# Second layer of a two-layer graph kernel: values stationary on column halves, normalisation on GpSimd, projections issued beside attention

## Chip, cores, metric

One core of one Trainium2 chip. The metric is the device time of one execution in microseconds (us); lower is better. The record marks each run as fast or slow; all runs quoted are marked fast.

## The reference

64 batches of 256 nodes with 512 features, fp32, one adjacency matrix for all. Each layer is x + f(relu(layernorm(x))), and the two layers follow each other:

```python
# layer 1 of the program ("first layer"): graph attention with additive logits, one head
Wh = h @ W
logits = leaky_relu(Wh @ a_src [rows] + Wh @ a_dst [columns], 0.2)
out = softmax(logits where adj else -inf) @ Wh
# layer 2 ("second layer"): masked attention, 8 heads of 64
q, k, v = h @ Wq.T + bq, h @ Wk.T + bk, h @ Wv.T + bv
scores = q @ k.T / 8, masked by adj
out = (softmax(scores) @ v) @ Wo.T + bo
```

## The kernel before

The kernel works on groups of two batches (4 tiles of 128 tokens), 32 groups. The first layer of the next group is issued among the second layer of this group. On each engine the program order is fixed when the kernel is built.

Names in the profiles: PE is TensorE, DVE VectorE, ACT ScalarE, POOL GpSimd, SP the engine that issues the transfers. `pw`, `pq`, `pk`, `pv` are the products with W, Wq, Wk, Wv; `po` the output products, and on its own line the first layer's value product; `pt` the transposes of the normalised x; `pp` those of probabilities; `psc` the scores; `pav` the second layer's values. A bank is one buffer of the `ps_` pools, to which TensorE writes its results. The parts that the change touches:

```python
ps_tr = ... tile_pool(name="ps_tr", bufs=3, space=PSUM)     # transposes
ps_sc = ... tile_pool(name="ps_sc", bufs=3, space=PSUM)     # scores
# ... cut ...
def values(t, hq, pr):                      # four heads of one tile
    # ... cut: pav is one bank of ps_mm, 128 tokens x 512 columns ...
    for i in range(2):
        pp = ps_tr.tile(...)
        # ... cut: transposes of two heads' probabilities into pp ...
        if i: nc.scalar.copy(pT, pp)
        else: nc.vector.tensor_copy(pT, pp)
        for r in range(2):
            h = hq * HQ + 2 * i + r
            for kc in range(NC):            # probabilities stationary, 64 columns of v move
                nc.tensor.matmul(pav[:, h*DH:(h+1)*DH], pT[:, r, kc, :],
                                 v[:, b*NC+kc, h*DH:(h+1)*DH], ...)

def finish(t):
    rc = 1 / sm                             # reciprocal sums, after the values
    nc.vector.tensor_mul(av, pav, rc ...)
    # ... cut: four transposes of av into pa, copy to aT ...
    project_rows(po, aT, wo_sb, 0)
    # ... cut: add to x, write out ...

for g in range(G):
    # ... cut ...
    for n, _ in enumerate(layer1(g)):       # norm, q, k, v, then attention of group g
        if n % 5 != 4:
            next(ahead, None)               # first layer of group g + 1
    run(ahead)
```

Of the kernel before, what the change touches and what calls it, by code (L numbers as in the profile page):

```python
# [8 lines left out]
F32 = mybir.dt.float32  # L9
# [15 lines left out]
def kernel(  # L25
# [17 lines left out]
    """Two pre-norm residual layers over batches of N nodes, kept on chip between them:  # L43
    graph attention with additive logits, then masked multi-head attention.

    A group is two batches, i.e. NT = 4 tiles of 128 tokens; its first layer is issued
    among the second layer of the group before it.
    """
# [17 lines left out]
    ps_tr = ctx.enter_context(tc.tile_pool(name="ps_tr", bufs=3, space=PSUM))  # L66
    ps_sc = ctx.enter_context(tc.tile_pool(name="ps_sc", bufs=3, space=PSUM))
# [47 lines left out]
    # 0 where there is an edge, MASKED where there is none  # L115
# [5 lines left out]
    def norm_relu_T(xt, g, layer):  # L121
        """relu(layernorm(x)) with the features on the partitions: [P, DC, TOK]."""
# [10 lines left out]
        yield  # L133
        hT = big.tile([P, DC, TOK], F32, tag="hT", name=f"hT{nm}")
        for t in range(NT):
            xn = work.tile([P, D], F32, tag="xn", name=f"xn{nm}_{t}")
            nc.vector.tensor_scalar(
                xn, xt[:, t, :], mv[:, t, 0:1], rstd[:, t : t + 1], op0=ALU.subtract, op1=ALU.mult
            )
            pt = ps_tr.tile([P, DC, P], F32, tag="tr", name=f"pt{nm}_{t}")  # L140
            for c in range(DC):
                nc.tensor.transpose(pt[:, c, :], xn[:, c * P : (c + 1) * P], ident)  # L142
            nc.scalar.activation(hT[:, :, t * P : (t + 1) * P], pt, AF.Relu)  # L143
            yield
        return hT

    def project_rows(dst, hT, w_t, t):
        """dst[tokens of tile t, all columns] = h @ w_t"""
# [5 lines left out]
    def project_T(dst, hT, w_t, e):  # L154
        """dst[columns of chunk e, all tokens] = (h @ w_t).T"""
# [5 lines left out]
    def layer0(g):  # L161
# [3 lines left out]
        wh = big.tile([P, NT, D], F32, tag="wh", name=f"wh_{g}")  # L165
        es = small.tile([P, NT], F32, tag="es", name=f"es_{g}")
        ed = small.tile([P, NT], F32, tag="ed", name=f"ed_{g}")
        for t in range(NT):
# [3 lines left out]
            for dst, a in ((ed, a_dst_b), (es, a_src_b)):  # L172
                junk = work.tile([P, D], F32, tag="junk", name=f"junk_{g}_{t}", bufs=2)
# [3 lines left out]
            yield  # L177

        prob, rec = {}, {}
        for b in range(GB):  # L180
# [22 lines left out]
            # a row without an edge gives 0  # L203
# [4 lines left out]
            yield  # L208

        for b in range(GB):  # L210
# [22 lines left out]
            yield  # L233

    def layer1(g):
        xt = groups.pop(g)
# [4 lines left out]
        qT = big.tile([P, DC, TOK], F32, tag="qT", name=f"qT_{g}", bufs=1)  # L241
        kT = big.tile([P, DC, TOK], F32, tag="kT", name=f"kT_{g}", bufs=1)
        v = big.tile([P, NT, D], F32, tag="v", name=f"v_{g}")
        for e in range(DC):
# [8 lines left out]
            yield  # L253
        for t in range(NT):
# [3 lines left out]
            if t % 2:  # L258
                yield

        HQ = 4
        state = {}

        def scores(t, hq):
            """Softmax numerators of four heads of tile t, tokens on the partitions."""
            b, c = divmod(t, NC)
            if hq == 0:
                state[t] = (
                    small.tile([P, HEADS], F32, tag="mx1", name=f"mx1_{g}_{t}"),
                    small.tile([P, HEADS], F32, tag="sm1", name=f"sm1_{g}_{t}"),  # L270
                )
            mx, sm = state[t]
            # heads of one parity share a bank: those of the other are on the other half of the rows
            psc = [
                ps_sc.tile([P, 2, N], F32, tag="sc", name=f"psc_{g}_{t}_{hq}_{r}") for r in range(2)
            ]
            for i in range(2):
                for r in range(2):
                    e = hq * 2 + i
                    rows = slice(r * DH, (r + 1) * DH)  # L280
                    nc.tensor.matmul(  # L281
                        psc[r][:, i, :],
                        qT[rows, e, t * P : (t + 1) * P],
                        kT[rows, e, b * N : (b + 1) * N],
                        start=True,
                        stop=True,
                    )
            s = work.tile([P, HQ, N], F32, tag="s", name=f"s_{g}_{t}_{hq}", bufs=2)
            for j in range(HQ):
                i, r = divmod(j, 2)  # L290
                h = hq * HQ + j
                nc.vector.tensor_tensor_reduce(  # L292
                    out=s[:, j, :],
                    in0=psc[r][:, i, :],
                    in1=mbias[:, c, :],
                    scale=1.0,
                    scalar=FLOOR,
                    op0=ALU.add,
                    op1=ALU.max,
                    accum_out=mx[:, h : h + 1],  # L300
                )
            hs = slice(hq * HQ, (hq + 1) * HQ)
            nmx = small.tile([P, HQ], F32, tag="nmx1", name=f"nmx1_{g}_{t}_{hq}")
            nc.vector.tensor_scalar_mul(nmx, mx[:, hs], -1.0)  # L304
            pr = work.tile([P, HQ, N], F32, tag="pr1", name=f"pr1_{g}_{t}_{hq}")
            for j in range(HQ):
                h = hq * HQ + j
                nc.scalar.activation(  # L308
                    pr[:, j, :], s[:, j, :], AF.Exp, bias=nmx[:, j : j + 1], accum_out=sm[:, h : h + 1]
                )  # L310
            return pr

        def values(t, hq, pr):
            b = t // NC
            if hq == 0:
                state[t] += (ps_mm.tile([P, D], F32, tag="mm", name=f"pav_{g}_{t}"),)
            pav = state[t][2]
            for i in range(2):
                pp = ps_tr.tile([P, 2, NC, P], F32, tag="tr", name=f"pp1_{g}_{t}_{hq}_{i}")
                for r in range(2):  # L320
                    for kc in range(NC):
                        nc.tensor.transpose(  # L322
                            pp[:, r, kc, :], pr[:, 2 * i + r, kc * P : (kc + 1) * P], ident
                        )
                pT = work.tile([P, 2, NC, P], F32, tag="pT1", name=f"pT1_{g}_{t}_{hq}_{i}")
                if i:
                    nc.scalar.copy(pT, pp)  # L327
                else:
                    nc.vector.tensor_copy(pT, pp)  # L329
                for r in range(2):  # L330
                    h = hq * HQ + 2 * i + r
                    for kc in range(NC):
                        nc.tensor.matmul(  # L333
                            pav[:, h * DH : (h + 1) * DH],
                            pT[:, r, kc, :],
                            v[:, b * NC + kc, h * DH : (h + 1) * DH],
                            start=(kc == 0),
                            stop=(kc == NC - 1),
                        )

        def finish(t):
            _, sm, pav = state.pop(t)
            rc = small.tile([P, HEADS], F32, tag="rc1", name=f"rc1_{g}_{t}")
            nc.vector.reciprocal(rc, sm)
            av = work.tile([P, HEADS, DH], F32, tag="av", name=f"av_{g}_{t}", bufs=2)
            nc.vector.tensor_mul(  # L346
                av,
# [77 lines left out]
```

## Time and profile before

| | before |
|---|---|
| time, median of 4 runs | 3982.99 us (3980.50 to 3984.59) |
| span of the profiled run | 3978.6 us |
| mean granted TensorE clock (1 is full speed) | 0.998 |
| TensorE busy | 97% |
| GpSimd busy | 6% |

The prediction below shows the busy line, the chain and TensorE's timeline. Here are, in addition, the waits of TensorE, from the groups of instructions of TensorE alone, each shape by itself. Columns: line, engine, operation, output<-inputs, shapes, count, then busy us and mean ns of one, then idle us of TensorE just before them and what ended it. And the row of the page with the granted clock in 40 slices.

```profile
PEclk9999999999999999999999999999999999999999
...
L281 PE MATMUL psc<-kT,qT 64*128 64x256 f32 x2048 | 399.0, 413 | 8.4 <-DVE mx L292 6.4
L142 PE MATMUL pt<-ident,xn 128*128 128x128 f32 x1024 | 139.8, 281 | 50.5 <-ACT hT L143 30.7 <-DVE xn L137 15.0 <-DVE mv L128 4.8
L354 PE MATMUL pa<-ident,av 128*128 128x128 f32 x512 | 84.4, 288 | 34.7 <-DVE av L346 33.8
L214 PE MATMUL pp<-ident,pr 128*128 128x128 f32 x256 | 41.3, 285 | 4.0 <-ACT pr L200 4.0
```

### The profile page before, as it was taken

Reading aid. Unit: us, or ns where it says so; the run is one execution under the profiler, and the core shown is the slowest. Engines: PE = TensorE matmul, PEld = TensorE weight load, DVE = VectorE, ACT = ScalarE, POOL = GpSimd, SP = SyncE. Lnnn points to the kernel's source line nnn. Section 1 sums busy time; section 2 is a strip of 40 time slices with the busy share of each in tenths; the row PEclk is TensorE's granted clock in tenths of the full one; section 3 lists DMA queues with packets and bytes.
Section 4 is the critical chain, followed back from the end, with each engine's and each line's share of the span. In section 5 each row is a group of like instructions: output and inputs, shape, how many; then the busy total and the mean of one; then the engine's idle time right before and its main releaser. Section 6 shows DMA issues by size and latency. Waiting matters only on the chain.

```text
span 3978.6 us, 41676 instructions
## 1 busy us (share of the span) xinstructions
PE 3853.1 (97%) x15744; PEld 2182.8 (55%) x15744; DVE 1732.9 (44%) x5186; ACT 1109.1 (28%) x3201; POOL 247.8 (6%) x206
## 2 busy tenths in 40 slices
PE   7999999999999999999999999999999999999999
PEld 3555555555555555555555555555555555555555
DVE  3444344443345433454334543344443444433442
ACT  1322223222233222332223322233222232222332
POOL 1000000000000000000000000000000000000000
PEclk9999999999999999999999999999999999999999
DMA  2000000000000000000000000000000000000000
GB/s 98 22 9 16 19 22 22 9 16 19 22 22 14 13 17 22 22 22 6 19 19 22 22 6 19 19 22 22 9 16 19 22 22 9 16 19 22 11 11 11
DMA packets 39144, 76.33 MB, mean 19 GB/s; under 512 B 3297, under 2 KB 3297, under 8 KB 38945
## 3 DMA queue, kind: packets, MB, share of 16 engines
q1 hardware_dynamic: 38480, 72.36, 5.0%
q8 instruction: 124, 2.03, 0.2%
q0 software_dynamic: 464, 1.32, 0.1%
q14 instruction: 76, 0.61, 0.1%
HBM read 40.11 MB, written 33.55 MB: 19 GB/s over the span
## 4 chain that ended last, share of the span: by engine, by line
PE 87%; DVE 9%; ACT 3%; issue 1%; DMA 0%; POOL 0%; POOLq 0%; DVEq 0%; ACTq 0%
PE pav L333 12%; PE po L150 12%; PE pq L157 11%; PE pw L150 11%; PE pv L150 11%; PE pk L157 11%; PE psc L281 5%; PE pp L322 5%; PE po L223 4%; ACT hT L143 2%; PE pa L354 2%; DVE s L292 2%; PE pt L142 2%; DVE av L346 2%; DVE x L230 1%; DVE junk L174 1%
## 5 line engine op out<-in xcount | busy, mean ns | idle before, releaser
L333 PEld LDWEIGHTS pav<-v,pT 128*128 128x128 f32 x4096 | 498.8, 191 | 136.5 <-issue 45.9
L308 ACT ACTIVATE pr<-s,nmx 128x256 f32<-128x256 f32 x1024 | 507.0, 497 | 180.1 <-DVE nmx L304 157.9
L333 PE MATMUL pav<-v,pT 128*128 128x64 f32 x4096 | 525.0, 276 | 6.9 <-DVE pT L329 4.8
L150 PE MATMUL po<-wo_sb,aT 128*128 128x512 f32 x1024 | 474.2, 606 | 3.2 <-ACT aT L356 0.7
L157 PE MATMUL pq<-hT,wq_sb 128*128 128x512 f32 x1024 | 463.6, 595 | 7.9 <-ACT hT L143 7.9
L157 PE MATMUL pk<-hT,wk_sb 128*128 128x512 f32 x1024 | 460.3, 592 | 0.0
L150 PE MATMUL pw<-w_sb,hT 128*128 128x512 f32 x1024 | 460.1, 592 | 0.0
L150 PE MATMUL pv<-wv_sb,hT 128*128 128x512 f32 x1024 | 444.7, 592 | 0.0
L252 DVE TENSOR_SCALAR kT<-pk,bk_c 128x512 f32<-128x512 f32 x128 | 96.1, 751 | 776.0 <-PE pk L157 776.0
L281 PE MATMUL psc<-kT,qT 64*128 64x256 f32 x2048 | 399.0, 413 | 8.4 <-DVE mx L292 6.4
L292 DVE CUSTOM_DVE_ANT_0 s<-psc,mbias 128x256 f32<-128x256 f32 x1024 | 384.3, 417 | 11.1 <-PE psc L281 6.8
L171 ACT COPY wh<-pw 128x512 f32<-128x512 f32 x128 | 74.9, 585 | 1100.2 <-PE pw L150 1100.2
L157 PEld LDWEIGHTS pk<-hT,wk_sb 128*128 128x128 f32 x1024 | 194.6, 190 | 244.9 <-issue 244.9
L150 PEld LDWEIGHTS pv<-wv_sb,hT 128*128 128x128 f32 x1024 | 194.6, 190 | 244.9 <-issue 244.9
L150 PEld LDWEIGHTS pw<-w_sb,hT 128*128 128x128 f32 x1024 | 194.7, 190 | 244.5 <-issue 244.5
L157 PEld LDWEIGHTS pq<-hT,wq_sb 128*128 128x128 f32 x1024 | 191.9, 190 | 245.2 <-issue 229.6
L322 PE MATMUL pp<-ident,pr 128*128 128x128 f32 x2048 | 311.6, 277 | 5.0
L327 ACT COPY pT<-pp 128x512 f32<-128x512 f32 x256 | 149.1, 582 | 581.1 <-PE pp L322 578.2
L150 PEld LDWEIGHTS po<-wo_sb,aT 128*128 128x128 f32 x1024 | 184.4, 190 | 217.3 <-issue 184.1
L322 PEld LDWEIGHTS pp<-ident,pr 128*128 128x128 f32 x2048 | 234.3, 145 | 83.6 <-issue 44.1
L281 PEld LDWEIGHTS psc<-kT,qT 64*128 64x128 f32 x2048 | 220.9, 185 | 100.1 <-issue 56.8
L174 DVE SCALAR_TENSOR_TENSOR junk<-wh,a_dst_b 128x512 f32<-128x512 f32 x128 | 88.5, 691 | 421.4 <-ACT wh L171 421.4
(57 smaller groups left out, 3103.3 us busy)
## 6 DMA issues: line engine op xcount, KB each, us to landing
x<-in_x_dram SPq DMA_DIRECT2D x64, 512.0 KB, 4.4
out_dram<-x SPq DMA_DIRECT2D x128, 256.0 KB, 2.0
w_sb<-in_L_gnn_W_dram SPq DMA_DIRECT2D x1, 1024.0 KB, 13.3
wq_sb<-in_L_gnn_Wq_dram SPq DMA_DIRECT2D x1, 1024.0 KB, 15.9
wk_sb<-in_L_gnn_Wk_dram SPq DMA_DIRECT2D x1, 1024.0 KB, 18.1
wv_sb<-in_L_gnn_Wv_dram SPq DMA_DIRECT2D x1, 1024.0 KB, 20.1
wo_sb<-in_L_gnn_Wo_dram SPq DMA_DIRECT2D x1, 1024.0 KB, 16.1
a_src_b<-in_L_gnn_a_src_dram POOLq DMA_DIRECT2D x1, 256.0 KB, 6.8
```

The source lines that it names most:

```text
L142: nc.tensor.transpose(pt[:, c, :], xn[:, c * P : (c + 1) * P], ident)
L150: nc.tensor.matmul(dst, hT[:, c, t * P : (t + 1) * P], w_t[:, c, :], start=(c == 0), stop=(c == DC - 1))
L157: nc.tensor.matmul(dst, w_t[:, c, e * P : (e + 1) * P], hT[:, c, :], start=(c == 0), stop=(c == DC - 1))
L174: nc.vector.scalar_tensor_tensor(junk, wh[:, t, :], 1.0, a, op0=ALU.mult, op1=ALU.mult, accum_out=dst[:, t : t + 1])
L223: nc.tensor.matmul(po, pT[:, mc, c * P : (c + 1) * P], wh[:, b * NC + mc, :], start=(mc == 0), stop=(mc == NC - 1),)
L252: nc.vector.tensor_scalar_add(kT[:, e, :], pk, bk_c[:, e : e + 1])
L281: nc.tensor.matmul(psc[r][:, i, :], qT[rows, e, t * P : (t + 1) * P], kT[rows, e, b * N : (b + 1) * N], start=True, stop=True,)
L292: nc.vector.tensor_tensor_reduce(out=s[:, j, :], in0=psc[r][:, i, :], in1=mbias[:, c, :], scale=1.0, scalar=FLOOR, op0=ALU.add, op1=ALU.ma ...
L308: nc.scalar.activation(pr[:, j, :], s[:, j, :], AF.Exp, bias=nmx[:, j : j + 1], accum_out=sm[:, h : h + 1])
L322: nc.tensor.transpose(pp[:, r, kc, :], pr[:, 2 * i + r, kc * P : (kc + 1) * P], ident)
L327: nc.scalar.copy(pT, pp)
L333: nc.tensor.matmul(pav[:, h * DH : (h + 1) * DH], pT[:, r, kc, :], v[:, b * NC + kc, h * DH : (h + 1) * DH], start=(kc == 0), stop=(kc == ...
```

## The change

Intent: take work off TensorE, which is the bound. (1) Values are stationary: 64 columns of v are loaded as weights, two heads on the two column halves of the array, and 256 columns of transposed probabilities move; the output comes out transposed, so the four transposes of `av` per tile go. (2) The output has tokens on the free axis, so the row sums can no longer be applied to it per partition; the probabilities are normalised before their transposes, on GpSimd, which is nearly idle. (3) q, k, v of the next group move into the stream issued beside attention, and the two streams are merged by estimated costs. One bank goes from transposes to scores.

```diff
-    ps_tr = ctx.enter_context(tc.tile_pool(name="ps_tr", bufs=3, space=PSUM))
-    ps_sc = ctx.enter_context(tc.tile_pool(name="ps_sc", bufs=3, space=PSUM))
+    ps_tr = ctx.enter_context(tc.tile_pool(name="ps_tr", bufs=2, space=PSUM))
+    ps_sc = ctx.enter_context(tc.tile_pool(name="ps_sc", bufs=4, space=PSUM))
 # ... cut: layer0(g) and the projections of layer1(g) become one generator dense(g) ...
+                nc.vector.reciprocal(rc, sm)
+                nc.gpsimd.tensor_tensor(
+                    pr,
+                    pr,
+                    rc.rearrange("p (h o) -> p h o", o=1).to_broadcast([P, HQ, N]),
+                    op=ALU.mult,
+                )
 # ... cut ...
                         nc.tensor.matmul(
-                            pav[:, h * DH : (h + 1) * DH],
-                            pT[:, r, kc, :],
+                            pav[r * DH : (r + 1) * DH, i, :],
                             v[:, b * NC + kc, h * DH : (h + 1) * DH],
+                            pTs[i, r][:, kc, :],
                             start=(kc == 0),
                             stop=(kc == NC - 1),
                         )
+            nc.scalar.copy(aTs[b][:, 2 * hq : 2 * hq + 2, :], pav)
 # ... cut: finish(b) without av, pa and their copy ...
+    DENSE_US, ATTENTION_US = 69.0, 39.2
+    def merge(first, second):               # always takes the stream that is behind
+        # ... cut ...
+        merge(attention(g), dense(g + 1) if g + 1 < G else iter(()))
```

## The prediction

> **What bounds the kernel now.** I read the page's busy line, then its chain of waits, then the costliest groups, then the timeline of TensorE in the middle of the run.
>
> ```profile
> PE 3853.1 (97%) x15744; PEld 2182.8 (55%) x15744; DVE 1732.9 (44%) x5186; ACT 1109.1 (28%) x3201; POOL 247.8 (6%) x206
> ...
> PE 87%; DVE 9%; ACT 3%; issue 1%; DMA 0%; POOL 0%; POOLq 0%; DVEq 0%; ACTq 0%
> ...
> L333 PE MATMUL pav<-v,pT 128*128 128x64 f32 x4096 | 525.0, 276 | 6.9 <-DVE pT L329 4.8
> ...
> L281 PE MATMUL psc<-kT,qT 64*128 64x256 f32 x2048 | 399.0, 413 | 8.4 <-DVE mx L292 6.4
> ```
>
> TensorE is busy 97% and carries 87% of the chain, GpSimd 6%. Only TensorE's time, or new waits of TensorE, can move the result. The clock view gives 0.998, so there is no throttling. Now the timeline of TensorE (start, length, count):
>
> ```profile
> 1883.13 0.70 PE L281 MATMUL psc<-kT,qT 64*128 64x256 f32 x2
> 1883.76 1.09 PE L322 MATMUL pp<-ident,pr 128*128 128x128 f32 x8
> 1884.78 0.70 PE L281 MATMUL psc<-kT,qT 64*128 64x256 f32 x4
> 1885.41 2.00 PE L333 MATMUL pav<-v,pT 128*128 128x64 f32 x16
> 1887.34 0.70 PE L281 MATMUL psc<-kT,qT 64*128 64x256 f32 x4
> 1888.20 0.66 PE L354 MATMUL pa<-ident,av 128*128 128x128 f32 x4 [0.15 <-DVE av L346]
> ...
> 1912.00 3.60 PE L157 MATMUL pk<-hT,wk_sb 128*128 128x512 f32 x8
> 1915.44 3.60 PE L157 MATMUL pq<-hT,wq_sb 128*128 128x512 f32 x8
> ```
>
> Differences of starts give prices. An fp32 matmul is two records. 512 columns: 3.43/8 = 0.429 us a record, 0.858 a matmul; 256 columns: half, 0.43 a matmul. A transpose: 1.02/8 = 0.128. A value record has 64 columns, yet 1.93/16 = 0.12: its 128-column weight load sets it. Scores: two records (one matmul) take 0.63 before the next operation starts, and four records on the two row halves take 0.63 too. So a pair shares the array, and a visit costs 0.43 per pair or unpaired matmul plus about 0.2.
>
> The period follows from a line that recurs:
>
> ```profile
> 115.10 1.13 PE L281 MATMUL psc<-kT,qT 64*128 64x256 f32 x8
> ...
> 1963.60 1.13 PE L281 MATMUL psc<-kT,qT 64*128 64x256 f32 x8
> ...
> 3919.91 4.14 PE L281 MATMUL psc<-kT,qT 64*128 64x256 f32 x20
> ```
>
> 1848.5 us is 15 groups, 123.2 us each. The head is 115 us, the last group's attention alone 59 us.
>
> **What the Trainium skill says.** "TensorE: Matmul & The Clock Gate", Part 3, measured speedup: three column tiles gave 2.38x, within some 5 ns of row tiling. The trace agrees for row halves (0.63 above); it has no column halves. "GPSIMD Engine Reference", 3.1: a two-input fp32 operation on 2048 elements takes 4497 ns; the trace has 1388 ns (median) for 512, so for 1024 I estimate 1.39 + 512 x (4.50-1.39)/1536 = 2.4 us. "SBUF — State Buffer", Who interferes with whom: VectorE and GpSimd share one port pair under an exclusive lock, which copies and tensor_scalar in SBUF and operations with two SBUF inputs need. The trace agrees: a four-element operation waited out a GpSimd one, 1.25 us instead of 0.17:
>
> ```profile
> 51.34 1.27 POOL L239 TENSOR_TENSOR x<-x,bo_b 128x512 f32<-128x512 f32 x1 [0.82 <-DVE xn L137]
> 51.38 1.25 DVE L130 TENSOR_SCALAR ve<-mv 128x4 f32<-128x4 f32 x1
> ```
>
> **The change part by part, TensorE us per group.** I counted the runs in the instruction order of both built programs.
> - Dense products w, q, k, v, o and the first layer's value product: 176 records before and after, 176 x 0.429 = 75.5.
> - Transposes except pa: 108 x 0.128 = 13.9, unchanged. The 16 of pa go: -2.1, and with them the wait for av (33.8 us in the whole run, 1.1 per group).
> - Values: 128 records x 0.12 = 15.4 become 32 matmuls of 256 columns. They alternate between the halves; if pairs overlap like the scores', the order gives 546 slots and 192 visits in the run: (546 x 0.43 + 192 x 0.2)/32 = 8.5. Gain 6.9.
> - Scores: before, three banks split the pairs: 672 slots, 415 visits, 11.6. After, four banks: 544 slots, 193 visits, 8.5. Gain 3.1.
> - Normalisation leaves VectorE's end (av, 0.69 a tile) for eight GpSimd multiplications of about 2.4 us, some 20 us of GpSimd per group. They lie between exponentials and transposes; the order puts one step of scores between, so their duration itself is mostly hidden.
> - q, k, v move into the next group's dense stream. TensorE must do them anyway; that only fills gaps.
>
> Work: before 75.5+16.0+15.4+11.6 = 118.5, against 123.2 measured, so 4.7 of waits and hand-overs. After 75.5+13.9+8.5+8.5 = 106.4.
>
> **The waits after**, followed by hand along the order with start-to-start times of the trace: mask-and-maximum step s 0.345 on VectorE, junk 0.62, z 0.40, z maximum and reduction 0.60 each, exponential 0.49 on ScalarE, copies 0.5 to 0.6.
> - *Start of the attention.* Four score banks are filled at once, and the next scores wait until VectorE has drained them; then transposes pt wait for hT copies, which stand behind eight exponentials (3.9 us) on ScalarE. TensorE gets 6.1 us of work done in 8.4: 2.3 lost.
> - *Second batch's scores beside the first layer's softmax.* After the last pw, VectorE has in line: 8 s (2.8), 2 junk (1.2), 4 z (1.6), two maxima and one reduction (1.8), small ones (0.4), so z's row maximum is ready at about 8.4, its exponential at 9.1. TensorE's next in order is a transpose of that very exponential, and it has 4.6 us of work until then: 4.5 to 4.8 lost. The second z maximum has two SBUF inputs and meets a GpSimd multiplication: 1 to 2 more. Waits for pT copies before the first layer's products and for row statistics, 1.5.
> - Remaining transpose and hand-over gaps 1.5, as before.
> Sum 2.3+4.7+1+1.5+1.5 = 11.0, so a group takes 117.4 us, -5.8. Of 12 us of work saved half comes back as waits.
>
> Total: head about 100 (115 less the four pw and the transposes that now come later), 31 x 117.4 = 3639, last attention alone about 55 (39 of work and the first chain through VectorE, ScalarE and GpSimd): 3794; the timed runs read 5.6 over the profile: 3800 us.
>
> **Rivals.**
> - *Full gain.* The waits stay at 4.7 as before: 111.1 per group, 3605 us. For it: the two streams are weighed by costs that sum to 108 us, so the writer expected this. Against it: the order above, in which TensorE cannot step over a blocked transpose.
> - *The halves don't overlap.* 32 matmuls x 0.43 plus 1.2 = 15 instead of 8.5: +6.5 a group, 4000 us. The pairs of the scores speak against it; nothing in this trace shows columns.
> - *The lock becomes the bound.* Each score step is followed by a four-element negation of the maxima, the form that lost 1.1 us at 51.38, and a multiplication runs for a sixth of the time. If the negations and z operations lose 1 to 2 us each on the path, the period is 121 to 124 and the time 3910 to 4000. Against it: VectorE's operation after the reciprocal starts 0.1 us later, before GpSimd takes the lock, so often GpSimd waits instead.
> - *GpSimd itself as the bound*: 20 + 7.7 us (247.8/32) of 117, no.
>
> **Range and chances.** The work is sure to some 2 us a group (60 us) if columns pair up, which I give 0.85; waits between 5 and 15 us move the time from 3610 to 3925. So 3640 to 3950 holds 8 in 10. Over 2% faster means below 3904: 0.77; within 2%: 0.20 (no pairing, or the lock); slower: 0.03.
>
> **What would show it.** Values: busy of pav near 270 us, and eight matmuls between two other operations in about 1.9 us; 3.6 if halves don't overlap. The pa group gone. Scores below 300 us. GpSimd multiplications near 2.4 us each, GpSimd busy about 850 us. The transposes of the first layer's probabilities with a wait of 3 to 5 us for the exponential in each group. VectorE records of the four-element negation and of the z maximum above 1 us where a multiplication runs. Period of a recurring line 115 to 120 us. Waits far below 9 us a group, or TensorE's share staying at 97%, would refute my hand-made chains; a period above 121 would mean the lock or the columns.

## The result

The changed kernel takes **3969.41 us** (median of 4, 3968.35 to 3970.40), the one before 3982.99 us on the same chip. The ratio is 0.9968, 95% interval 0.9953 to 0.9982. Ratios are taken from the record, which forms them from all fast runs of both kernels, so they are not quite the ratio of the medians quoted (here 0.9966). Work was taken away, and nearly no time went with it.

The page of the changed kernel: clock row, busy times, the chain that ended last, and the group of the new multiplications.

```profile
PE 3625.0 (91%) x13184; PEld 1858.3 (47%) x13184; DVE 1751.7 (44%) x5186; ACT 1112.7 (28%) x3201; POOL 762.2 (19%) x462
...
PEclk8999999999999999999999999999999999999999
...
PE 77%; DVE 12%; ACT 8%; issue 1%; POOL 1%; DMA 0%; ACTq 0%; DVEq 0%; POOLq 0%
...
L312 POOL TENSOR_TENSOR pr<-pr,rc 128x1024 f32<-128x1024 f32 x256 | 515.8, 2019 | 3011.6 <-DVE rc L311 2677.0
```

TensorE is no longer the whole story: 91% busy, 77% of the chain. Note that the clock row shows almost the same digits as before. A digit 9 is anything from 0.9 up, and the mean granted clock is 0.956 against 0.998. The page's row hides what turned out to be the cause.

Groups of TensorE, to be held against those above:

```profile
L150 PE MATMUL pw<-w_sb,hT 128*128 128x512 f32 x1024 | 504.0, 644 | 0.0
L279 PE MATMUL psc<-kT,qT 64*128 64x256 f32 x2048 | 335.1, 401 | 57.0 <-DVE mx L293 57.0
...
L350 PE MATMUL pav<-pT,v 128*64 128x256 f32 x2048 | 279.8, 390 | 0.7 <-DVE pT L344 0.7
...
L142 PE MATMUL pt<-ident,xn 128*128 128x128 f32 x1024 | 161.7, 298 | 56.7 <-DVE xn L137 29.1 <-ACT hT L143 27.3 <-DVE mv L128 0.3
L215 PE MATMUL pp<-ident,pr 128*128 128x128 f32 x256 | 64.1, 362 | 177.4 <-ACT pr L201 177.4
```

The values fell from 525.0 to 279.8 us, and the pa group is gone. The transposes of the first layer's probabilities now wait 177.4 us in the run, 5.5 a group (4.0 in all before). And pw, the same 1024 records as before, went from 592 to 644 ns each: unchanged work became slower.

### The profile page after: what moved, and what is told of

It is laid out like the page before. It is cut to its first block, busy times and chain, and to the rows that moved or that the text cites. A ratio compares the mean times of both kernels' runs of the same rounds, so it can differ in the third digit from the quotient of the medians.

```text
span 3967.7 us, 37119 instructions
## 1 busy us (share of the span) xinstructions
PE 3625.0 (91%) x13184; PEld 1858.3 (47%) x13184; DVE 1751.7 (44%) x5186; ACT 1112.7 (28%) x3201; POOL 762.2 (19%) x462
## 4 chain that ended last, share of the span: by engine, by line
PE 77%; DVE 12%; ACT 8%; issue 1%; POOL 1%; DMA 0%; ACTq 0%; DVEq 0%; POOLq 0%
PE pw L150 12%; PE pq L157 11%; PE pv L150 11%; PE pk L157 11%; PE po L150 8%; PE pav L350 7%; PE pp L335 6%; ACT pr L307 6%; PE po L224 5%; PE pt L142 3%; DVE s L293 3%; DVE st L127 2%; PE psc L279 2%; DVE nmx L197 1%; DVE x L231 1%
## 5 line engine op out<-in xcount | busy, mean ns | idle before, releaser
L312 POOL TENSOR_TENSOR pr<-pr,rc 128x1024 f32<-128x1024 f32 x256 | 515.8, 2019 | 3011.6 <-DVE rc L311 2677.0
L150 PE MATMUL pw<-w_sb,hT 128*128 128x512 f32 x1024 | 504.0, 644 | 0.0
L150 PE MATMUL po<-wo_sb,aT 128*128 128x512 f32 x1024 | 460.6, 593 | 0.0
L150 PE MATMUL pv<-wv_sb,hT 128*128 128x512 f32 x1024 | 453.0, 595 | 0.0
L279 PE MATMUL psc<-kT,qT 64*128 64x256 f32 x2048 | 335.1, 401 | 57.0 <-DVE mx L293 57.0
L335 PE MATMUL pp<-ident,pr 128*128 128x128 f32 x2048 | 313.5, 295 | 12.2 <-ACT pT L342 3.2
L150 PEld LDWEIGHTS pw<-w_sb,hT 128*128 128x128 f32 x1024 | 206.9, 211 | 248.4 <-issue 248.4
L335 PEld LDWEIGHTS pp<-ident,pr 128*128 128x128 f32 x2048 | 253.3, 151 | 127.1 <-issue 66.5
L224 PE MATMUL po<-wh,pT 128*128 128x512 f32 x512 | 266.0, 668 | 25.5 <-DVE pT L219 25.5
L350 PE MATMUL pav<-pT,v 128*64 128x256 f32 x2048 | 279.8, 390 | 0.7 <-DVE pT L344 0.7
L256 DVE TENSOR_TENSOR v<-pv,bv_b 128x512 f32<-128x512 f32 x128 | 88.6, 692 | 428.7 <-PE pv L150 428.7
```

The lines of the kernel that those rows point to most:

```text
L150: nc.tensor.matmul(dst, hT[:, c, t * P : (t + 1) * P], w_t[:, c, :], start=(c == 0), stop=(c == DC - 1))
L224: nc.tensor.matmul(po, pT[:, mc, c * P : (c + 1) * P], wh[:, b * NC + mc, :], start=(mc == 0), stop=(mc == NC - 1),)
L279: nc.tensor.matmul(psc[c, r][:, i, :], qT[rows, e, t * P : (t + 1) * P], kT[rows, e, b * N : (b + 1) * N], start=True, stop=True,)
L312: nc.gpsimd.tensor_tensor(pr, pr, rc.rearrange("p (h o) -> p h o", o=1).to_broadcast([P, HQ, N]), op=ALU.mult,)
L335: nc.tensor.transpose(pp[:, kc, c * P : (c + 1) * P], prs[c][:, 2 * i + r, kc * P : (kc + 1) * P], ident,)
L350: nc.tensor.matmul(pav[r * DH : (r + 1) * DH, i, :], v[:, b * NC + kc, h * DH : (h + 1) * DH], pTs[i, r][:, kc, :], start=(kc == 0), stop= ...
```

## Where the time went: half clock

The timeline of TensorE in one group of the changed kernel (start, length, group; in brackets the wait before it):

```profile
1852.93 2.92 PE L279 MATMUL psc<-kT,qT 64*128 64x256 f32 x16 [0.98 <-DVE mx L293]
1861.46 0.48 PE L215 MATMUL pp<-ident,pr 128*128 128x128 f32 x1 [5.61 <-ACT pr L201]
...
1864.48 4.66 PE L224 MATMUL po<-wh,pT 128*128 128x512 f32 x8
...
1873.27 3.70 PE L224 MATMUL po<-wh,pT 128*128 128x512 f32 x8 [0.78 <-DVE pT L219]
```

Eight records of 512 columns take 3.70 us at 1873, and the same eight take 4.66 us at 1864, some 3 us after a wait of 5.61 us. The view by windows gives busy time and granted clock in any stretch; the stretches here are laid on the edges at which the clock changed:

```profile
1852.96:1856.38 3.42, 2.89 (x16) 1.00 0.00 0
1856.38:1859.79 3.41, 0.00 (x0) 1.00 0.00 0
1859.79:1863.21 3.42, 1.75 (x8) 0.50 0.00 0
1863.21:1866.62 3.41, 3.27 (x9) 0.50 0.01 2
1866.62:1870.03 3.41, 3.41 (x16) 1.00 0.00 0
```

Columns: stretch, length, TensorE busy (instructions), granted clock, DMA. One stretch of 3.41 us without any matmul is followed by two stretches of 3.41 us at exactly half clock. A second place, at the start of each group's dense work:

```profile
1825.66:1829.07 3.41, 1.64 (x10) 1.00 0.00 0
1829.07:1832.48 3.41, 3.41 (x8) 0.50 0.00 0
1832.48:1835.90 3.42, 3.42 (x9) 1.00 0.00 0
```

Here TensorE was busy 1.64 of 3.41 us, and one stretch of half clock followed, over fully busy pw records. The Trainium skill, "TensorE: Matmul & The Clock Gate", Part 1, says the clock is halved after an idle window, and that the window is 4096 cycles at 1.2 GHz (3413 ns) and free-running. The trace agrees with the length and with the two states (1.00 and 0.50); the clock records of all 17 traces show that every half-clock stretch lasted 1, 2, 3 or 4 times 3.4133 us (but the last of each run, which its end cuts off), and in each run that has many of them all began within 0.01 us of one phase of a 3.4133 us grid. But it did not take an idle window here: one that was 0.48 busy was followed by half clock as well.

What this costs in a group is an estimate from these lines. In the stretch at 1829 the pw records start 0.85 us apart, behind it 0.43, so half clock doubles the time of work. At the first place 1.75 + 3.27 us are busy at half clock, so half of it, 2.5 us, is lost; at the second 3.41 / 2 = 1.7 us. Together 4.2 us a group.

**The period.** Outputs are written once a group, so their issue times mark the groups. Two marks ten groups apart, for the changed kernel:

```profile
1515.34 50.83 SPq L366 DMA_DIRECT2D out_dram<-x  x4
...
2744.14 50.83 SPq L366 DMA_DIRECT2D out_dram<-x  x4
```

1228.80 / 10 = 122.880 us a group. That is 36.00 times 3.4133 us. The single groups run 122.29, 122.66, 122.79, 122.83, 122.86, 122.87, 122.88, 122.88: they settle on that value. The kernel before does not: its groups take a steady 123.23 us, 36.10 windows, with one half-clock stretch in the whole middle of the run. A loop whose period is not a whole number of windows drifts against the grid of windows; whether, and how much of, the half clock hits it depends on where it stands; so a position at which loop and windows keep step can hold itself. I call that locked to the windows. How it holds itself is an argument; what the runs show is the settling and the experiments of the third and fourth round.

## The experiments

Each ran with three rounds against the kernel before on the same chip. "Group" is the mean distance of output marks over groups 5 to 25, and "windows" that over 3.4133 us. The rounds ran on three chips; the kernel before took 3981 to 3983 us in all of them.

| kernel | time, us | ratio to before | clock | group, us | windows |
|---|---|---|---|---|---|
| before | 3983 | 1 | 0.998 | 123.30 | 36.12 |
| changed | 3969.4 | 0.9968 | 0.956 | 122.88 | **36.00** |
| e_nonorm | 3876.9 | 0.9734 | 0.968 | 120.00 | 35.16 |
| e_late | 4079.0 | 1.0241 | 0.956 | 126.29 | **37.00** |
| e_best1 | 3968.9 | 0.9964 | 0.971 | 122.88 | **36.00** |
| e_warm | 3966.4 | 0.9958 | 0.978 | 122.72 | 35.95 |
| e_dve | 3964.8 | 0.9958 | 0.957 | 122.88 | **36.00** |
| e_warm2 | 4081.4 | 1.0248 | 0.996 | 126.27 | 36.99 |
| e_oldissue | 3966.4 | 0.9961 | 0.968 | 122.88 | **36.00** |
| e_newissue | 4076.3 | 1.0238 | 0.988 | 126.10 | 36.94 |
| a_pad4 | 3972.9 | 0.9978 | 0.970 | 122.88 | **36.00** |
| b_pad4 | 4034.6 | 1.0132 | 0.998 | 124.95 | 36.61 |
| e_keep | 4014.7 | 1.0085 | 0.983 | 124.36 | 36.43 |
| e_best4 | 3756.6 | 0.9459 | 0.963 | first 119.47, then 113.8 and 118.3 in turn | **35.00**, then **68.00** for two groups |
| a_pad8 | 4079.3 | 1.0244 | 0.957 | 126.29 | **37.00** |
| a_pad12 | 4083.5 | 1.0255 | 0.971 | 126.29 | **37.00** |
| e_best6 | 3691.1 | 0.9269 | 0.995 | 113.82 | 33.35 |

### First round: the wait and the multiplication

First theory (A): the long wait for the first layer's exponential, with the slow clock behind it, ate the gain. Rival (B): GpSimd's multiplication, through the memory port it shares with VectorE, ate it.

**e_nonorm**: the multiplication is taken out (wrong result).

```diff
-                nc.gpsimd.tensor_tensor(pr, pr, rc..., op=ALU.mult)
```

> The changed kernel without the GpSimd multiplication (the result is wrong on purpose). Theory A (TensorE waits in its fixed order for the first layer's exponential, and its clock is halved after the wait): only the part of the wait that the port lock makes goes. In the changed kernel's trace the two-element negation took 1.85 us instead of 0.16 and the second row maximum 0.99 instead of 0.68, so the wait of 5.6 us a group falls to about 3.6, and the clock loss behind it may shrink with it: 2 to 4.5 us a group, 3830 to 3905 us. Theory B (the lock is what ate the gain): the wait falls below 1 us, and with the clock loss 8 us a group go: 3720 us or less.

Measured 3876.9 us. The same group of transposes as above:

```profile
L215 PE MATMUL pp<-ident,pr 128*128 128x128 f32 x256 | 60.9, 348 | 112.0 <-ACT pr L201 111.9
```

The wait shrank by 2.0 us a group, and half clock remained (0.968). Taking the multiplication out is worth 92 us, not the whole gap. How it acts on the wait shows in VectorE's timeline of the changed kernel (all engines, cut to these rows):

```profile
1856.26 4.48 POOL L312 TENSOR_TENSOR pr<-pr,rc 128x1024 f32<-128x1024 f32 x2 [17.81 <-DVE rc L311]
...
1858.00 0.99 DVE L194 SCALAR_TENSOR_TENSOR z<-z 128x512 f32<-128x512 f32 x1
1858.92 1.85 DVE L197 TENSOR_SCALAR nmx<-nmx 128x2 f32<-128x2 f32 x1
1860.81 0.51 ACT L201 ACTIVATE pr<-z,nmx 128x256 f32<-128x256 f32 x1 [3.00 <-DVE nmx L197]
```

An operation on two elements took 1.85 us, until GpSimd was done, and the exponential that TensorE waits for stood behind it. Over the run this operation took 978 ns on average, against 162 ns in the kernel before and 163 ns in e_nonorm. In this stretch it is the port lock that the prediction named and feared (a different thing from the lock to the clock's windows below).

**e_late**: the merge is replaced by a fixed order, in which the first layer's value products stand after more of the attention.

```diff
-  ... soft0 soft1 pp0_0 V01 pp0_1 stat1 pt1_0 pt1_1 pt1_2 F0 pt1_3 ...
+  ... soft0 soft1 V01 F0 pp0_0 pp0_1 stat1 pt1_0 pt1_1 pt1_2 pt1_3 ...
   (S scores, V values, F output product of batch, half; pp0 first layer's value product;
    stat1, pt1 statistics and transposes of the second norm)
```

> The changed kernel with one thing moved in the order of issue: the first layer's probability transposes and value products come after the attention's next value step and output product, which are ready. Theory A: the wait for the first layer's exponential (177 us of TensorE's idle time in the run) falls below 30 us, the half clock behind it goes (granted clock at least 0.975), 5.6 + 2.3 us a group: about 3724 us. Theory B (the lock delays VectorE wherever the work stands): the wait turns up elsewhere, 3900 us or more.

Measured 4079.0 us, a miss by far for theory A; theory B's number, 3900 us or more, came out. The wait for the exponential was gone, and another took its place, since nothing was left to fill the time after the first layer's product:

```profile
1799.43 7.13 PE L224 MATMUL po<-wh,pT 128*128 128x512 f32 x16 [0.51 <-DVE pT L219]
1811.22 2.95 PE L142 MATMUL pt<-ident,xn 128*128 128x128 f32 x12 [4.65 <-DVE xn L137]
```

**e_best1**: another fixed order, with the next group's norm first and attention work between the statistics and the second norm.

```diff
+  stat0 pt0 S00 pw0 pw1 S01 pw2 V00 pw3 S10 soft0 soft1 V01 F0 pp0_0 pp0_1 S11 stat1 V10 pt1 qk0 ...
```

> As e_late, and the next group's first normalisation and its transposes are issued before the attention's first scores, and other products between the row statistics and the second normalisation's transposes. Theory A: the waits at the start of the attention (2.7 us) and the half clock behind them (1.5 us) shrink too: 3724 less 31 x 3.5 = about 3615 us, granted clock 0.985 or more. Theory B: above 3880 us.

Measured 3968.9 us: again a miss for theory A and within theory B's number. Neither run shows that B's cause was at work; e_dve below takes the port lock away. The waits at the start of attention were less (17.2 us in the run for the scores instead of 57.0), but the second batch's scores and the first layer's softmax still met on VectorE and ScalarE. The copies of transposed probabilities stood behind them, and the second layer's transposes waited 168 us in the run instead of 12.2. Two windows of half clock followed in each group that I sliced.

**e_warm**: the changed kernel with five useless products (ten records, 4.3 us) issued in the wait before the first layer's transposes.

```diff
+            if b == 0 and g > 0:
+                for _ in range(5):
+                    nc.tensor.matmul(pp..., ident, wh[:, NT - 1, :], start=True, stop=True)
```

> The changed kernel with five useless 512-column products (4.3 us of TensorE) added for every group in the middle of the wait for the first layer's exponential; the result stays right. If the half clock after that wait costs what the trace shows (about 2.3 us a group), the kernel with MORE work is faster: 3969 - 31 x 2.3 = about 3898 us, granted clock about 0.975. If only the waiting itself counts, the time stays at 3969 or grows.

Measured 3966.4 us: 133 us more TensorE work (31 x 4.3) cost nothing, and the clock was 0.978 as in the first reading, but the gain of 71 us did not come; by its time the second reading ("stays at 3969") fits. The marks say more: over most of this run the groups take 122.0 and 123.7 us in turn, and two of them 72.00 windows, so this loop too keeps step with the windows, two groups at a time. Where half clock was sliced, the window before it was still only 0.48 to 0.58 busy.

### Second round: the parts

**e_dve**: the normalisation on VectorE (right result).

```diff
-                nc.gpsimd.tensor_tensor(
+                nc.vector.tensor_tensor(
```

> The multiplication of the probabilities by the reciprocal sums moves from GpSimd to VectorE (right result). A 128x512 multiply-add of VectorE on the same memory took 0.82 us, so a 128x1024 one is estimated at 1.2 to 1.6 us, 8 a group, about 11 us more of VectorE a group, which is 44% busy. If the loss is that GpSimd's 2.0 us operations hold VectorE up at the shared memory, VectorE's own price is lower than the hold and the time falls to 3900-3950 us, with the one-column operation behind the first layer's maxima back near 0.16 us. If instead any normalisation ahead of the transposes costs the same wherever it stands, 3960-4010 us.

Measured 3964.8 us: in the second range (3960-4010), a miss for the first. The multiplication took 1218 ns on VectorE:

```profile
L312 DVE TENSOR_TENSOR pr<-pr,rc 128x1024 f32<-128x1024 f32 x256 | 311.8, 1218 | 3.3
```

The two-element operation was back at 161 ns, so the hold at the shared port was gone; the longer time was not. That does not yet show that normalising costs the same wherever it stands: the group is 122.88 us again, and only the next round explains why.

**e_warm2**: more useless products.

```diff
-                for _ in range(5):
+                for _ in range(8):
+            if layer == 0 and g > 0 and t > 1:      # ahead of the norm's last two tiles
+                for _ in range(2):
+                    nc.tensor.matmul(pt..., ident, w_sb[:, 0, :], start=True, stop=True)
```

> Eight useless 512-column products (3.4 us at full clock) fill the wait before the first layer's transposed probabilities whole, and two more stand ahead of each of the last two transposed tiles of the first layer's norm. If half clock after waits is real lost time, the granted clock rises to 0.985 or more, the first products po after the wait come back from 5.1 to 3.4 us for eight, and the time is 3890-3930 us in spite of about 5 us more TensorE work a group. If the clock in the records costs nothing, or the waits just move on, 3955-3990 us.

Measured 4081.4 us with clock 0.996, outside both ranges. Half clock can be driven out, as expected. But eight products are 6.9 us and not the 3.4 of the expectation, and the 744 useless records are 10.0 us a group (744 x 0.429 / 32) and not 5; TensorE's waits fell only from 9.7 to 4.9 us a group, so half of it and more lengthened the group. Its 36.99 windows are a coincidence, not the lock: between its marks 5 and 25 there is no half clock that could hold it.

**e_oldissue**: parts 1 and 2 without part 3: q, k, v ahead of their own attention, with the issue rule of before.

```diff
-        merge(attention(g), dense(g + 1) ...)
+        for n, _ in enumerate(layer1(g)):           # norm, q, k, v, attention(g)
+            if n % 5 != 4:
+                next(ahead, None)                   # layer0(g + 1)
```

> The column-half values and GpSimd's normalisation stay; the third part is undone: q, k, v are issued ahead of their own group's attention again, with the next group's first layer among both. Theory: the third part puts the first layer's chain (maxima, exponentials, transposes, update, statistics) on the path with too little TensorE work beside it; without it the waits shrink to some 5 us a group, TensorE's 107 us of work show, and the time is 3650-3780 us. Rival: the lock and the values' own copies cost it, whatever the issue: 3900 us or more.

Measured 3966.4 us, in the rival's range. The third part alone is not what eats the gain: without it the waits stand elsewhere (2.20 us for GpSimd's product ahead of the second layer's transposes) and half clock follows there.

```profile
1846.28 0.38 PE L333 MATMUL pp<-ident,pr 128*128 128x128 f32 x1 [2.20 <-POOL pr L310]
1846.64 1.56 PE L277 MATMUL psc<-kT,qT 64*128 64x256 f32 x4
```

**e_newissue**: part 3 alone, with the attention of before.

```diff
 # open merge as changed; scores(t, hq), values(t, hq, pr), finish(t) as before
+                yield 1.05   # scores
+                    yield 3.0    # values
+                        yield 4.0    # output product
```

> The third part alone: the attention of the kernel before (values with the probabilities stationary, normalised after the values), in the new issue order. TensorE work is that of before, 118.5 us a group. Theory: the new order brings its waits of 6 us a group or more and slow clock after them, so 4030-4130 us. Rival: the new order is neutral or helps, and the loss is in the values and their normalisation: 3940-3990 us.

Measured 4076.3 us, in the range of the theory, but mostly not by its mechanism: waits were 3.5 us a group against 2.6 before, while the score records went from 399.0 to 483.0 us busy; in the order of the trace they are split into 542 visits (uninterrupted runs of score matmuls) instead of 415.

```profile
L284 PE MATMUL psc<-kT,qT 64*128 64x256 f32 x2048 | 483.0, 415 | 38.3 <-DVE mx L295 38.3
```

Part 3 alone costs time. Most of its groups take a steady 125.70 us, so its mean of 36.94 windows is no lock either.

### Third round: is the period locked?

At this point five kernels stood at 3965 to 3970 us and three at 4076 to 4081, whatever had been done to them, and the output marks of five of these eight gave 36.00 or 37.00 windows (e_warm 72.00 for two groups; e_warm2 and e_newissue are only near 37). Theory: the loop is locked to the windows of the clock. Rival: half clock is only a consequence of waits, and added work costs its own length.

**a_pad4**: the changed kernel with two useless products (four records, 1.72 us) a group in the middle of the dense stretch, where nothing waits. The order of all other TensorE instructions is the same. **b_pad4**: the same two products in the kernel before.

```diff
             pv = ps_mm.tile([P, D], F32, tag="mm", name=f"pv_{g}_{t}")
+            if t == 1:
+                for _ in range(2):
+                    nc.tensor.matmul(pv, ident, w_sb[:, 0, :], start=True, stop=True)
```

> The changed kernel with two useless 512-column products (four records, 4 x 0.429 = 1.72 us, right result) ahead of one value projection of each group, in the middle of the dense stretch where TensorE waits for nothing; the order is otherwise the same. In the changed kernel, and in three variants of different work, the period of a group settles at 122.88 us, which is 36 times 3.4133 us. Theory: the clock is set by windows of that length, and the loop has locked to them, so that the work hides in the loss: 122.88 us a group and 3965-3973 us, with a higher granted clock. Rival: half clock is only a consequence of waits and the coincidence means nothing: 32 x 1.72 = 55 us more, 4024 us.

> Control: the same two products at the same place of the kernel before, which has no half clock. Both theories expect 55 us more here: 4037 us (4030-4045), period 124.95 us.

b_pad4 took 4034.6 us, 53.5 more than before: work costs its length (55 worked out). a_pad4 took 3972.9 us, 3.5 more than the changed kernel. The output marks of a_pad4 ten groups apart:

```profile
1517.29 50.83 SPq L369 DMA_DIRECT2D out_dram<-x  x4
...
2746.07 50.83 SPq L369 DMA_DIRECT2D out_dram<-x  x4
```

122.878 us a group: still 36 windows. What took the work in is visible: of the two places with half clock only the one behind the long wait is left in the slices of a_pad4,

```profile
1858.30:1861.71 3.41, 0.00 (x0) 1.00 0.00 0
1861.71:1865.12 3.41, 1.68 (x8) 0.50 0.00 0
1865.12:1868.54 3.42, 3.28 (x9) 0.50 0.04 7
```

and pw is back at 599 ns a record. The theory held, the rival (4024) fell. One caution: 1.72 us is, to 0.02 us, what one fully busy window at half clock loses (1.71). A length that is no multiple of it would have been a sharper test, and none was run.

**e_keep**: the useless products reduced to where TensorE waits, six before the transposes and one in the first norm.

```diff
-                for _ in range(5):
+                for _ in range(6):
+            if layer == 0 and g > 0 and t == 2:
+                dm = ps_mm.tile([P, D], F32, tag="mm", name=f"dm_{g}")
+                nc.tensor.matmul(dm, ident, w_sb[:, 0, :], start=True, stop=True)
```

> The changed kernel with useless products only where TensorE waits: six (5.1 us) ahead of the first layer's transposed probabilities, where the wait is 5.6 us, and one between the first two and the last two transposed tiles of the first layer's norm, so that no window of 3.41 us is less than about 0.6 busy. Theory: no half clock at all (granted clock 0.995 or more), the loop comes free of the windows, and the period is its own one without half clock, estimated from the five-product run as 120.3 us with perhaps 1 us more: 3880-3915 us. Rival (the waits move elsewhere, nothing is gained by the clock): 3955-3985 us.

Measured 4014.7 us, a miss of both ranges. The order of the scores and transposes moved as well, the transposes pt waited 88 us in the run instead of 57, and half clock stayed, behind windows with TensorE busy 0.43 to 0.67 of the time. Filling with useless work did not get the kernel free at a profit.

**e_best4**: real work in the waits. The values of the first batch stand between the last pw and the first layer's transposes, the output product of the first batch between the statistics and the projections; the copies of the second layer's transposed probabilities all go to ScalarE.

```diff
+  S00 S01 V00 V01 S10 F0 S11 V10 V11 F1          (attention)
+  stat0 pt0 S00 pw0 pw1 S01 pw2 pw3 soft0 soft1 V00 V01 pp0_0 pp0_1 stat1 S10 F0 pt1
+  qk0 S11 qk1 V10 qk2 qk3 V11 v0 F1 v1 v2 v3     (merged)
-                    if r:
-                        nc.scalar.copy(pT, pp)
-                    else:
-                        nc.vector.tensor_copy(pT, pp)
+                    nc.scalar.copy(pT, pp)
```

> A fixed order that fills the two long latencies of the first layer with the attention's own work: both value steps of the first batch stand between its last product pw and its transposed probabilities, and the output product of the first batch between its row statistics and the next projections; the copies of transposed probabilities all go to ScalarE. If the latencies are covered, waits fall to some 5 us a group, no half clock follows, and the time is 3660-3760 us. If new waits for the copies take their place with half clock after them, 3860-3970 us.

Measured 3756.6 us (four runs: 3755.7, 3756.2, 3757.1 and 3799.0). The time is in the first range, but half clock did follow, with a clock of 0.963 in the profiled run and 0.976 in the others: the number came out, the reasoning only in part. The profiled run is the longest of the four. In it groups 2 to 13 take 119.47 us, 35.00 windows, with four windows of half clock each; from then on groups take 113.8 and 118.3 us in turn:

```profile
1820.85 54.73 SPq L363 DMA_DIRECT2D out_dram<-x  x4
1939.18 54.71 SPq L363 DMA_DIRECT2D out_dram<-x  x4
2052.97 54.71 SPq L363 DMA_DIRECT2D out_dram<-x  x4
```

Two groups are 232.12 us, 68.00 windows, and every second group has three windows of half clock (the first from 1909.1 to 1919.4). So this is not freedom, but a second lock, over two groups. That the three faster runs were in it for longer is likely, but not traced.

### Fourth round: how far does the lock reach, and can it be left?

From a_pad4, the group without half clock is 122.88 - 1.72 - 2.5 = 118.7 us, where 2.5 is half of the 4.96 us busy in its two windows. From the changed kernel it is 122.88 - 4.2 = 118.7 as well.

**a_pad8** and **a_pad12**: four and six useless products at the place of a_pad4.

> The changed kernel with four useless products (eight records, 3.43 us) a group in the dense stretch. From the run with 1.72 us the group without half clock is estimated at 122.88 - 1.72 - 2.5 (two windows at half clock, 0.73 busy) = 118.7 us. With 3.43 us it is 122.1, still below 36 windows, 122.88. Theory: still locked or nearly, 3970-3990 us. Rival (work costs its own length): 3969 + 110 = 4079 us.

> The same with six useless products (5.15 us). The group without half clock is then estimated at 123.9 us, more than 36 windows, so the lock at 36 cannot hold: theory 4000-4080 us, period between 123.9 and 126.3 (37 windows), not 122.88. Rival: 3969 + 165 = 4134 us; if a lock at 36 held nevertheless, 3970 us, and the estimate of 118.7 would be wrong.

a_pad8 took 4079.3 us: outside the theory's range, and the rival's number (4079). Its marks:

```profile
1556.14 50.83 SPq L369 DMA_DIRECT2D out_dram<-x  x4
...
2819.06 50.83 SPq L369 DMA_DIRECT2D out_dram<-x  x4
```

1262.92 / 10 = 126.292 us, 37.00 windows. This run alone can't tell lock from rival, since the 3.43 us added are one window (3.413) to 0.02 us: its clock, its two places of half clock and the way its period settles are those of the changed kernel, one window later. a_pad12 took 4083.5 us, 3.5 over the theory's range, far from the rival (4134), and has the same 126.29, in the range for the period. The rival is also 51 us off at a_pad4. So the time is a staircase: 0, 1.72, 3.43 and 5.15 us of added work a group gave 3969, 3973, 4079 and 4084 us. The slices say why the step came earlier than I expected. a_pad8 has both places of half clock (4.2 us), a_pad12 only the first (2.5 us):

| kernel | group | added work | half clock | group without both |
|---|---|---|---|---|
| changed | 122.88 | 0 | 4.2 | 118.7 |
| a_pad4 | 122.88 | 1.7 | 2.5 | 118.7 |
| a_pad8 | 126.29 | 3.4 | 4.2 | 118.7 |
| a_pad12 | 126.29 | 5.15 | 2.5 | 118.6 |

The four runs give the same 118.7 us to 0.1. At 3.43 us of added work a lock at 36 windows would have needed a loss of 0.8 us, and losses of that size were not seen in these slices; 122.1 + 4.2 is 37 windows. I had assumed that the loss could take any size, and that was wrong.

**e_best6**: e_best4 with the second score step one product earlier, since in the first half of e_best4's run a 2.1 us wait for the sums `junk` had brought four windows of half clock.

```diff
-  stat0 pt0 S00 pw0 pw1 S01 pw2 pw3 soft0 ...
+  stat0 pt0 S00 pw0 S01 pw1 pw2 pw3 soft0 ...
```

> As the fixed order before, with the second score step one product pw earlier, so that its exponentials and its GpSimd multiplications are over when the copies and the sums of the last two projected tiles come due; there TensorE waited 2.1 us, which brought four windows of half clock in the first half of that run (period 119.47 = 35 windows) and none in the second (113.8 and 118.3 in turn). If that wait goes, the period is the free one all along, some 113 us, and the time 3610-3680 us. If the wait moves elsewhere, 3740-3800 us.

(The expectation says that e_best4's second half has no half clock; as shown above, it has three windows in every second group.) Measured **3691.1 us** (3689.6 to 3691.7), ratio 0.9269, right result. It beats both kernels, the one before by 7.3%, and the changed one by 7.0% by the medians of their own rounds. Its page:

```profile
PE 3568.8 (97%) x13184; PEld 1804.6 (49%) x13184; DVE 1662.4 (45%) x4930; ACT 1223.4 (33%) x3457; POOL 727.2 (20%) x462
...
PE 68%; DVE 20%; ACT 8%; issue 2%; POOL 1%; DMA 0%; ACTq 0%; DVEq 0%; POOLq 0%
```

The same 13184 TensorE records as in the changed kernel, now in groups of 113.8 us, with the clock at 0.995 and no half clock between the groups. The time is somewhat above the expected 3610 to 3680: the largest wait left is one of 1.7 us for a ScalarE copy before the last pw.

```profile
1942.11 3.70 PE L150 MATMUL pw<-w_sb,hT 128*128 128x512 f32 x8 [1.70 <-ACT wh L172]
```

Order and ScalarE copies changed together in e_best4 and e_best6; what each is worth alone was not measured.

## Why the prediction was wrong

**Right: the work of the values.** It expected pav near 270 us, 1.9 us for eight matmuls, and the pa group gone. Measured were 279.8 us, and 16 records (eight matmuls) at 1869.95 with the next operation at 1871.83, 1.88 us. The column halves do overlap.

**Nearly right: scores and GpSimd.** Scores were expected below 300 us; they are at 335.1 busy. A multiplication took 2.02 us instead of the estimated 2.4, and GpSimd was busy 762 us instead of 850.

**Right: the waits, with one detail missed.** It named the transposes of the first layer's probabilities with 3 to 5 us a group (5.5 measured), the port lock meeting z's maximum, and the start of the attention. But z's maximum took 1.00 us at most and the four-element negation 0.70 (median 0.16), not above 1 us; what was held up to 1.86 us was the two-element operation behind z's maximum. Added up from the timeline over four groups in the middle, the waits are 9.7 us a group; 11.0 were expected, 1.5 of them hand-overs.

**Right: the work saved, and nearly the group.** Before, a group is 123.2 us with 2.6 of waits, so 120.6 of work; after, it is 118.7 without half clock (four runs) with 9.7 of waits, so 109.0. That is 11.6 us saved; the sum of prices said 118.5 - 106.4 = 12.1. (Both are 2.1 to 2.6 us above the sums of prices, perhaps for hand-overs between operations. Of small slips: 108 x 0.128 is 13.8, not 13.9; VectorE's listed work sums to 7.8 where 8.4 is used; and the 5.6 us added for timed runs were 1.8 here. None matters.) "So a group takes 117.4 us": 118.7, as far as work and waits go.

**The step that failed**: "The clock view gives 0.998, so there is no throttling", together with costing each wait at its own length. The clock of the kernel before was carried over to one whose waits are of another kind: before, 2.6 us a group in short pieces; after, one piece of 5.6 us and a cluster that leaves TensorE busy only 48% of a window. In its place the runs showed half clock behind both: the mean clock fell to 0.956, and these two places cost 4.2 us a group, by the estimate above, on top of their own length. Of the 169 us between 3800 and 3969, 31 x 4.2 = 130 are this, and 31 x 1.3 = 40 are the group; head and tail were right (3967.7 - 31 x 122.88 = 158 against 155 predicted).

**The rivals.** "The lock becomes the bound" gave 3910 to 4000 with a group of 121 to 124 us, and both numbers came out so, for another reason: with the port lock removed (e_dve) the group was 122.88 us again. Reading the matching number as proof of that rival would have been wrong. The text also said "a period above 121 would mean the lock or the columns"; it meant neither, so the list of what could show the prediction wrong lacked the true cause.

**Where the gain went.** In us a group: work -11.6, waits +7.0 (2.6 to 9.7), half clock +4.2. The sum is -0.4, which is 123.2 to 122.9, and all that the time saw. Given enough work in the waits, the same TensorE records take 113.8 us (e_best6, waits 2.4 us a group).

**Open.** What share of busy time keeps a window from half clock. Laid on the grid of each run's clock edges, in the 13 runs with repeated half clock, every window that TensorE spent at full clock and less than 0.40 busy was followed by it, and none over 0.70 busy was; between, both happened (0.69 followed in e_newissue, 0.44 not in e_late), and the kernel before has one case at 0.77. So the busy share in the records alone does not decide; transposes and half-array products are in these windows, and they may count differently. The price of the shared memory port by itself: e_nonorm takes it away together with the normalisation (92 us), and in e_dve the lock to the windows hides it. Whether added work of other lengths is absorbed too. And what each of the new order and ScalarE's copies is worth in e_best6.

## What to carry to other kernels

Before a change that trades TensorE work for waits, look at how long the single waits are and how they lie, not at their sum: here a wait of 5.6 us and a window that was half empty (0.48 busy) were paid twice, and the remedy was real work in the wait, fixed in the order. If variants with different work come out at the same time, divide the period of the loop, and that of two groups, by 3.413 us: at a whole number the loop may be locked, if there is half clock in each period (e_warm2 stood at 36.99 without any); then small gains and small losses can be invisible, and useless work added in a busy stretch, of a length that is no multiple of half a window, tells it apart from a true bound. And look at the mean granted clock itself: a row of nines hides 4%.

## What the Trainium skill lacked or had wrong

- "TensorE: Matmul & The Clock Gate", Part 1, gives an idle window as what half clock comes after. Here a window in which TensorE was busy 1.64 of 3.41 us (0.48) was followed by it too, and in e_keep one at 0.67. A later section of that page has frequent short idles do the same; what share of idle time it takes, no page says.
- The same page, "HAM oscillation", tells the cost of half clock after waits, but not that a loop can lock to the windows: 122.88 us = 36.00 windows in five kernels with different work or order, 126.29 = 37.00 in three more, 68.00 and 72.00 for two groups in e_best4 and e_warm; 1.72 us of added work a group cost 3.5 us in the run instead of 55; 3.43 us, about a window, cost the whole 110. No page has this.
- Its Part 4 says that transposes do not count as busy in the same way, without a figure. No run here separates that; in e_warm, half clock followed windows at 0.58 busy that contain transposes and score products.
- "GPSIMD Engine Reference", 3.1, gave by interpolation an estimate of 2.4 us for 1024 elements; a multiplication with a broadcast operand took 2.02 us (256 of them). The page has no figure for a broadcast operand.
